# Recurrence of a bidirectional decay scan: the order of TensorE's transposes and matmuls, and of ScalarE's copies, within one iteration

## The chip, the cores and the metric

The kernel runs on one core of one Trainium2 chip. The metric is device microseconds of one execution; the time of a kernel is the median of several runs. The core has a matmul engine (TensorE, PE in the profile; PEld is its weight load), VectorE (DVE), ScalarE (ACT), GpSimd (POOL) and SyncE (SP), which issues most DMAs. Each engine works through its own instructions in order; semaphores tie them together. TensorE writes to PSUM banks, which the other engines read.

## The reference, cut to what matters

The computation is a gated bidirectional recurrence over 1024 tokens, on 4 sequences of 1024 channels, followed by two blocks of attention over 16 slots. Only the recurrence is touched.

```python
ek = exp(min(k, 30)); ekv = ek * k                    # v is k here
a[t] = a[t-1] * decay + ekv[t];  b[t] = b[t-1] * decay + ek[t]     # forward
# the same backward in time, giving nf, df, nb, db
num = nf + nb - ekv + exp(min(u + k, 30)) * k
den = df + db - ek  + exp(min(u + k, 30))
x = sigmoid(r) * (num / max(den, 1e-8)) * (0.8 + 0.2 * tf)
```

The first slot block needs, of each row of x, its sum of squares and its products with 16 vectors, and x itself in both layouts (tokens by channels, and turned).

## The kernel before, in words

The recurrence works on blocks of 128 channels by 1024 tokens, channels on partitions: `N = B * NK = 32` iterations, `i` over 4 sequences of 8 blocks. The loop is software-pipelined: iteration `i` holds the scans of block `i`, the quotient of block `i-1` and the transposes of block `i-2`. Nearly every instruction is pinned to program order (`pin`), so the order written in the loop is the order on each engine.

What each engine does in iteration `i`, in its order before the change:

- VectorE: forward scan of `ek` into the denominator half of `both[i]` (L320), forward scan of `ekv` into the numerator half (L320), backward scan of the denominator (L320, "both<-columns,edges,both"; it starts from `edge[0]`), the sum with the own term (L361, `den_sum`, needs `own[i]`), the quotient of block i-1 (L458, `newton`, needs `num_ps[i-1]` complete in PSUM), the own numerator (L374), and the backward scan of the numerator over pairs of tokens (L417, `numerator`, needs `pairs[i]` in PSUM and `edge[1]`).
- GpSimd: two products of block i-1 with its quotient guess (L447, L448), clamp and product for block i+1 (L302, L308), the floor of the denominator (L411, needs L361), and the last product of block i-1 into the gate (L471, needs L458).
- ScalarE: `own[i]` (L312), the two edges (L333: multiplications of one column; `edge[0]` from the end of the first scan, `edge[1]` from the end of the second), the copies of transposed blocks out of PSUM (L497, L529), the issue of the row store (L506), the quotient guess (L432 Ln, needs L411; L434 Exp), `ek` of block i+2 (L292), the square of block i-1 (L474) and the next decay matrix (L391).
- TensorE: transposes of block i-2 in two halves (L496, four 128x128 each), products of the squares of block i-2 (L482 "raw<-quo"), a block of weight work (L528 transposes, or L536 products, one item of the list `projection`), the pairs (L398, L399), the products of block i-1 (L482 "raw<-gate", needs L471), sometimes a half of a late transpose, and last the three sums of the numerator of block i (L382, `add_pairs`).

Every transposed half, every weight block and the pairs go through the same PSUM tile (`tag="ptr", bufs=1`), so each has to be read out by ScalarE (or, for the pairs, by L417) before the next is written. `own` and `num` have one PSUM buffer each as well; `both` has two, so the first scan of iteration i+1 waits until block i-1's L471 has read its buffer.

`HK = 4`: in iterations with `i % 4 == 0` the gates of four blocks go through one sigmoid (L279, 128x4096, with a table load on each side), and no transposes are done; the two halves that are left out are turned late, in the two iterations after the next. In iterations with `i % 4 == 1` there is a weight block and no late half, with 2 and 3 there are both. Iterations up to 3 have fewer blocks, as nothing is there yet.

## Time and profile before

| what | value |
|---|---|
| median of 3 runs | 1105.29 us (1103.33, 1105.29, 1107.35) |
| the profiled execution | 1108.89 us, of which the profiled span is 1107.1 us |
| busy in the span | PE 1002.8, PEld 552.3, VectorE 739.5, ScalarE 516.7, GpSimd 549.2 us |
| recurrence, first to last L417 | 20.31 to 406.94 us |
| idle of VectorE before L417 | 32.3 us in 15 places |
| idle of GpSimd before L447 in 87 to 394 us | 13.0 us |
| idle of TensorE before "raw<-gate" (L482) in 87 to 394 us | 34.1 us |

The span is what the profiler saw of one execution, 1.8 us shorter than that execution's time. "Busy" is a union of instruction times on an engine; durations of neighbours overlap by some tens of ns, so start-to-start distances are used where instructions follow each other. The table's first two rows are different executions: the profiled one took 3.6 us more than the median.

### The profile page before, as it was taken

How to read it: one execution, taken by the hardware profiler on the slowest of the kernel's cores; microseconds unless marked ns; L12 is line 12 of the kernel's file. 1: busy time of each engine (PE TensorE's matmuls, PEld its weight loads, DVE VectorE, ACT ScalarE, POOL GpSimd, SP SyncE). 2: the span in 40 equal slices, each digit the busy share in tenths (PEclk: the TensorE clock that was granted, in tenths of full speed). 3: DMA queues.
4: the chain of work that ended last, by engine and by line, in shares of the span. 5: the costliest groups of instructions: out<-in, count | busy, mean ns of one | idle time of the engine just before them, and what ended most of it. 6: DMA issues, size and time to landing. Idle time of an engine off the chain costs nothing.

```text
span 1107.1 us, 12203 instructions
## 1 busy us (share of the span) xinstructions
PE 1002.8 (91%) x4218; PEld 552.3 (50%) x4218; DVE 739.5 (67%) x1049; ACT 516.7 (47%) x818; POOL 549.2 (50%) x417
## 2 busy tenths in 40 slices
PE   4678888987888897899999999999899999999996
PEld 1223232322323242484666666765584667676764
DVE  7898898989898986233666656565233555555555
ACT  6576777667686753012343434334113333333332
POOL 4999898989898972200222222222100343444444
PEclk9899898989899899899999999999999999999999
DMA  8575464747464345591477777562771355555554
GB/s 271 177 258 190 144 212 136 262 138 247 152 209 120 108 139 200 168 407 59 169 265 256 262 283 271 204 207 99 270 288 40 142 200 193 206 190 209 190 203 158
DMA packets 121790, 218.81 MB, mean 198 GB/s; under 512 B 10928, under 2 KB 76592, under 8 KB 121728
## 3 DMA queue, kind: packets, MB, share of 16 engines
q1 hardware_dynamic: 87872, 199.15, 51.0%
q10 hardware_dynamic: 33280, 16.78, 5.1%
q0 software_dynamic: 576, 2.10, 0.5%
q8 instruction: 33, 0.54, 0.2%
q14 instruction: 29, 0.24, 0.1%
HBM read 150.90 MB, written 67.11 MB: 197 GB/s over the span
## 4 chain that ended last, share of the span: by engine, by line
PE 74%; DVE 12%; POOL 7%; ACT 3%; issue 2%; DMA 1%; SPq 1%; POOLq 0%; DVEq 0%; ACTq 0%
PE psc L1146 20%; PE po L1203 19%; DVE both L320 8%; PE raw L482 7%; PE num L382 4%; POOL gate L471 3%; PE ptr L1134 3%; PE pk L1006 3%; PE pkv L936 3%; PE pv L1074 2%; PE ptr L496 2%; DVE both L417 2%; PE pairs L398 2%; PE pw L886 1%; POOL both L411 1%
## 5 line engine op out<-in xcount | busy, mean ns | idle before, releaser
L1146 PE MATMUL psc<-km,xt 128*128 128x272 f32 (+1 forms) x1024 | 238.4, 386 | 0.0
L1203 PE MATMUL po<-vm,e 128*128 128x512 f32 x512 | 230.4, 593 | 0.9 <-ACT e L1193 0.9
L1146 PEld LDWEIGHTS psc<-km,xt 128*128 128x128 f32 x1024 | 189.5, 190 | 29.1
L1180 POOL TENSOR_TENSOR e<-e,den 128x256 f32<-128x256 f32 x64 | 40.6, 634 | 252.4 <-DVE den L1178 231.3
L1203 PEld LDWEIGHTS po<-vm,e 128*128 128x128 f32 x512 | 94.8, 190 | 95.7 <-issue 85.4
L482 PE MATMUL raw<-gate,lhs 128*32 128x512 f32 x128 | 74.7, 712 | 47.9 <-POOL gate L471 47.8
L1244 DVE SCALAR_TENSOR_TENSOR y<-y,inv,npost_bc 128x1024 f32<-128x1024 f32 x62 | 79.7, 1285 | 41.3 <-POOL inv L1239 41.3
L1212 DVE TENSOR_TENSOR y<-po,y 128x512 f32<-128x512 f32 x128 | 85.8, 674 | 31.0 <-PE po L1203 30.8
L1232 ACT ACTIVATE junk<-y 128x1024 f32<-128x1024 f32 x63 | 66.7, 1059 | 69.3 <-DVE y L1244 69.1
L447 POOL TENSOR_TENSOR both<-both,quo 128x1024 f32<-128x1024 f32 (+1 forms) x33 | 76.1, 2305 | 21.7 <-ACT quo L434 21.2
L1239 POOL TENSOR_TENSOR inv<-mean,minus_half 128x1 f32<-128x1 f32 x64 | 35.6, 557 | 96.7 <-DVE mean L1237 96.7
L382 PE MATMUL num<-both,ident 128*128 128x512 f32 x128 | 73.8, 702 | 6.3 <-DVE both L320 4.3
L308 POOL TENSOR_TENSOR ekv<-ek,kf 128x1024 f32<-128x1024 f32 (+1 forms) x33 | 76.1, 2308 | 2.6
L448 POOL TENSOR_TENSOR gate<-gate,quo 128x1024 f32<-128x1024 f32 (+1 forms) x33 | 76.9, 2329 | 0.0
L1193 ACT COPY e<-pet 128x256 f32<-128x256 f32 x64 | 23.8, 372 | 113.0 <-PE pet L1192 112.9
L320 DVE TENSOR_TENSOR_SCAN both<-columns,edges,both 128x1024 f32<-128x1024 f32 x32 | 74.4, 2325 | 1.8 <-ACT edges L333 1.8
L471 POOL TENSOR_TENSOR gate<-gate,both 128x1024 f32<-128x1024 f32 x31 | 73.7, 2377 | 1.1
L320 DVE TENSOR_TENSOR_SCAN both<-columns,ek 128x1024 f32<-128x1024 f32 (+1 forms) x32 | 71.8, 2243 | 3.5 <-POOL gate L471 3.3
L1341 POOL TENSOR_TENSOR y<-y,xin 128x1024 f32<-128x1024 f32 x31 | 73.1, 2359 | 1.4 <-DVE y L1244 1.4
L320 DVE TENSOR_TENSOR_SCAN both<-columns,ekv 128x1024 f32<-128x1024 f32 (+1 forms) x32 | 71.4, 2231 | 0.0
L1137 ACT COPY xt<-ptr 128x512 f32<-128x512 f32 x64 | 37.0, 577 | 70.2 <-PE ptr L1134 70.2
L1237 DVE TENSOR_SCALAR mean<-total 128x1 f32<-128x1 f32 x64 | 9.8, 154 | 85.2 <-ACT junk L1232 45.8
(212 smaller groups left out, 1639.8 us busy)
## 6 DMA issues: line engine op xcount, KB each, us to landing
y<-rows SPq DMA_DIRECT2D x64, 512.0 KB, 4.3
kf<-in_ft_dram SPq DMA_DIRECT2D x32, 512.0 KB, 5.3
gate<-in_xt_dram SPq DMA_DIRECT2D x32, 512.0 KB, 6.9
turned_rows<-gate SPq DMA_DIRECT2D x32, 512.0 KB, 3.6
xt<-turned_rows SPq DMA_DIRECT2D x32, 512.0 KB, 5.7
rows<-y SPq DMA_DIRECT2D x32, 512.0 KB, 2.9
xin<-in_x_dram SPq DMA_DIRECT2D x32, 512.0 KB, 4.6
rows<-stage ACTq DMA_DIRECT2D x31, 512.0 KB, 4.2
```

The lines of the kernel that those rows point to most:

```text
L308: pin(nc.gpsimd.tensor_tensor(ekv[:, part], ek[:, part], kf[:, part], ALU.mult))
L320: nc.vector.tensor_tensor_scan(dst[:, way], dec, src[:, way], start, ALU.mult, ALU.add)
L382: nc.tensor.matmul(num_ps[:, ts(h, 512)], by, src, start=False, stop=True, skip_group_check=True)
L447: pin(nc.gpsimd.tensor_tensor(den, den, quo[:, part], ALU.mult))
L448: pin(nc.gpsimd.tensor_tensor(xk, xk, quo[:, part], ALU.mult))
L471: pin(engine.tensor_tensor(xk, xk, factor[:, part], ALU.mult))
L482: nc.tensor.matmul(raw[rows_b, ts(h, 512)], lhs[:, w].rearrange("p h s -> p (h s)"), src[:, ts(h, 512)], start=(k == 0 and w == k), stop=( ...
L1146: nc.tensor.matmul(psc[g][:, :n], xt_g[g][:, k, :], maps["km"][:, g // NT, k, :n], start=(k == 0), stop=(k == NK - 1),)
L1203: nc.tensor.matmul(po, et[:, ts(c, P)], vm[:, c, ts(h, 512)], start=(c == 0), stop=(c == 1),)
L1212: pin(nc.vector.tensor_add(half, po, half))
L1244: pin(nc.vector.scalar_tensor_tensor(y[g], y[g], inv[g], npost_bc, ALU.mult, ALU.mult))
L1341: pin(nc.gpsimd.tensor_add(y[g - 1], y[g - 1], xin[g - 1]))
```

## The change

All edits lie in the loop of the recurrence. `sums_a` is split into `sums` (the two forward scans), `make_edge` and `denominator`; the transposes, weight blocks and their copies become pairs of closures, of which the first issues TensorE's part and returns the copy.

TensorE's order in an iteration with `i % 4 != 0` becomes: first half of block i-2, sum 0 and sum 1 of `num_ps[i-1]`, second half, sum 2, a third block (late half, or none), squares half 0, a fourth block (weights), squares half 1, pairs of block i, products of block i-1. The three sums (L382) move from the end of iteration i-1 to the beginning of iteration i, and the late half from the end of an iteration into the third place of the next. With `i % 4 == 0`: the three sums, the squares, the pairs, the products, as before.

ScalarE's order with `i % 4 != 0` becomes: copy 0, square of block i-2, `edge[0]`, copy 1 and the issue of the row store, `own[i]`, copy 2, `edge[1]`, copy 3, decay matrix of block i+1, guess (Ln, Exp), `ek` of block i+2. Before, it was: decay matrix, `own[i]`, `edge[0]` (those two exchanged with `i % 4 == 1`), late copy, `edge[1]`, copies 0 and 1, row store, weight copy, guess, `ek`, square. With `i % 4 == 0`: square, `own`, `edge[0]`, the sigmoid, `edge[1]`, decay matrix, guess.

VectorE's and GpSimd's orders are the same as before, and so is SyncE's; the gate loads of SyncE with `i % 4 == 3` wait for the late half, which stands later now.

```diff
+            adds = add_pairs(num_ps[i - 1], flat[i - 1], by[i - 1]) if past else [lambda: None] * 3
+            if i % HK == 0:
+                for fill in adds:
+                    fill()
+                if older:
+                    square(i - 2, quo[i - 2])
+                own_exp(i, kf[i], own[i])
+                make_edge(i, both[i], edge[i], 0)
...
+                gates(i // HK)
+                if past:
+                    make_edge(i, both[i], edge[i], 1)
+                    late_stage = staged(i - 2)
+                    contract(i - 2, quo[i - 2], NK)
+            else:
...
+                if older:
+                    stage = staged(i - 2)
+                    blocks = [rows_block(i - 2, h, stage) for h in range(2)]
+                if i > HK and i % HK > 1:
+                    blocks.append(rows_block(i - i % HK - 2, i % HK - 2, late_stage))
+                if i >= 3 and projection:
+                    blocks.append(projection.pop(0))
+                blocks = blocks[:2] + [None] * (4 - len(blocks)) + blocks[2:]
...
+                turn_block(0)
+                adds[0]()
+                copy[0]()
+                if older:
+                    square(i - 2, quo[i - 2])
+                adds[1]()
+                make_edge(i, both[i], edge[i], 0)
+                turn_block(1)
+                adds[2]()
+                copy[1]()
+                own_exp(i, kf[i], own[i])
+                turn_block(2)
+                if older:
+                    contract(i - 2, quo[i - 2], NK, (0,))
+                copy[2]()
+                make_edge(i, both[i], edge[i], 1)
+                turn_block(3)
+                if older:
+                    contract(i - 2, quo[i - 2], NK, (1,))
+                copy[3]()
+            denominator(i, both[i], edge[i])
+            if i < N - 1:
+                pairs[i] = make_pairs(i, both[i], by[i])
+            if i + 1 < N - 1:
+                by[i + 1] = decay_matrix(i + 1)
...
-            if older:
-                now = i % HK > 0
-                stage = staged(i - 2)
-                for h in range(2):
-                    if now:
-                        copy = turn_half(i - 2, h)
-                    contract(i - 2, quo[i - 2], NK, (h,))
-                    if now:
-                        copy(stage)
...
-            if i >= 3 and i % HK and projection:
-                projection.pop(0)()
-            if i < N - 1:
-                pairs[i] = make_pairs(i, both[i], by[i])
...
             if past:
-                square(i - 1, quo[i - 1])
-            if i + 1 < N - 1:
-                by[i + 1] = decay_matrix(i + 1)
-            if past:
                 contract(i - 1, gate_of(i - 1), (i - 1) % NK)
...
-            add_pairs(num_ps[i], flat[i], by[i])
```

The new helper that issues a half and returns its copy (the row store goes out with the second half):

```diff
+        def rows_block(i, h, stage):
+            def turn():
+                xk = gate_of(i)
+                ptr = rec_ps.tile([P, 4, P], F32, tag="ptr", bufs=1, name=f"ptr_{i}_{h}")
+                for q in range(4):
+                    pin(nc.tensor.transpose(ptr[:, q, :], xk[:, ts(4 * h + q, P)], ident))
+                return lambda: copy(ptr)
+
+            def copy(ptr):
+                pin(nc.scalar.copy(stage[:, 4 * h : 4 * h + 4, :], ptr))
+                if h == 1:
+                    send(i, stage)
+
+            return turn
```

More of the change, by code (lines that the diff above doesn't have):

```diff
@@ L323, in scan, with sums @@
             )
-        def sums_a(i, ek, ekv, parts, own_exp, between):
-            b, k = i // NK, i % NK
+        def sums(i, ek, ekv, parts):
             flat = rec.tile([P, 2 * L + 2], F32, tag="both", bufs=2, name=f"both_{i}")
             both = flat[:, : 2 * L].rearrange("p (n t) -> p n t", n=2)
-            edge = [edges[:, i % 8, :], flat[:, 2 * L : 2 * L + 1]]
-            def make_edge(n):
-                pin(nc.scalar.mul(edge[n], both[:, n, L - 1 : L], turn[:, b, k : k + 1]))
-            late = i % HK == 1
-            if not late:
-                own_exp()
             for n, src in enumerate((ek, ekv)):
@@ L345, in sums_a, with make_edge, denominator @@
                     )
-                if n == 0:
-                    make_edge(0)
-            if late:
-                own_exp()
-            if i == 0:
-                make_edge(1)
-            between()
-            if i > 0:
-                make_edge(1)
+            return flat, both, [edges[:, i % 8, :], flat[:, 2 * L : 2 * L + 1]]
+        def make_edge(i, both, edge, n):
+            b, k = i // NK, i % NK
+            pin(nc.scalar.mul(edge[n], both[:, n, L - 1 : L], turn[:, b, k : k + 1]))
+        def denominator(i, both, edge):
             den = both[:, 0, :]
             scan(den, den, i, edge[0], True)
-            return both, edge[1], flat
         def den_sum(both, own):
@@ L404, in add_pairs @@
             later = flat[:, L + 2 :].rearrange("p (s h) -> p h s", h=2)[:, 0]
-            add(num_ps, 0, f[:, 0])
-            add(num_ps, 1, f[:, 1])
-            add(num_ps, 1, later, by)
+            return [
+                lambda: add(num_ps, 0, f[:, 0]),
+                lambda: add(num_ps, 1, f[:, 1]),
+                lambda: add(num_ps, 1, later, by),
+            ]
         def floor(both):
@@ L417, in numerator @@
                 nc.vector.tensor_tensor_scan(
-                    even[:, ::-1], dec, pairs[:, ::-1], edge, ALU.mult, ALU.add
+                    even[:, ::-1], dec, pairs[:, ::-1], edge[1], ALU.mult, ALU.add
                 )
@@ L424, in numerator_half @@
             num = both[:, 1, ts(h, 512)]
-            scan(num, num, i, edge if h else both[:, 1, 512:513], True)
+            scan(num, num, i, edge[1] if h else both[:, 1, 512:513], True)
         def guess(i, both, parts=(every,)):
@@ L489, in contract @@
                 )
-        def turn_half(i, h):
-            xk = gate_of(i)
-            ptr = rec_ps.tile([P, 4, P], F32, tag="ptr", bufs=1, name=f"ptr_{i}_{h}")
-            for q in range(4):
-                pin(nc.tensor.transpose(ptr[:, q, :], xk[:, ts(4 * h + q, P)], ident))
-            return lambda stage: pin(nc.scalar.copy(stage[:, 4 * h : 4 * h + 4, :], ptr))
+        def rows_block(i, h, stage):
[10 more added lines that the diff above has]
+            return turn
         def staged(i):
@@ L528, in turn_weights @@
                 pin(nc.tensor.transpose(ptr[:, q, :], part[:, ts(q, P)], ident))
-            pin(nc.scalar.copy(part.rearrange("p (q c) -> p q c", c=P), ptr))
+            return lambda: pin(nc.scalar.copy(part.rearrange("p (q c) -> p q c", c=P), ptr))
         def group_products(j2):
@@ L543, in group_products @@
                     )
-            pin(nc.scalar.copy(wo_next[j2][:, :, :P], acc[:, :2, :]))
+            return lambda: pin(nc.scalar.copy(wo_next[j2][:, :, :P], acc[:, :2, :]))
         def group_sums():
@@ L553, in group_sums @@
                 )
-            pin(nc.scalar.copy(wo_cw.rearrange("p j s -> p (j s)"), pc))
+            return lambda: pin(nc.scalar.copy(wo_cw.rearrange("p j s -> p (j s)"), pc))
         projection = []
@@ L580 @@
         by[0] = decay_matrix(0)
-        late_copy = None
         for i in range(N):
@@ L588 @@
             own[i] = rec_ps.tile([P, L], F32, tag="own", bufs=1, name=f"own_{i}")
-            both[i], edge[i], flat[i] = sums_a(
-                i,
-                ek[i],
-                ekv[i],
-                [every] if past else halves,
-                lambda: own_exp(i, kf[i], own[i]),
-                lambda: gates(i // HK) if i % HK == 0 else late_copy() if late_copy else None,
-            )
-            late_copy = None
+            flat[i], both[i], edge[i] = sums(i, ek[i], ekv[i], [every] if past else halves)
@@ new lines, with turn_block @@
+            adds = add_pairs(num_ps[i - 1], flat[i - 1], by[i - 1]) if past else [lambda: None] * 3
[6 more added lines that the diff above has]
+                make_edge(i, both[i], edge[i], 0)
+                if i == 0:
+                    make_edge(i, both[i], edge[i], 1)
[5 more added lines that the diff above has]
+            else:
+                blocks = []
+                if older:
[6 more added lines that the diff above has]
+                blocks = blocks[:2] + [None] * (4 - len(blocks)) + blocks[2:]
+                copy = [None] * 4
+                def turn_block(n):
+                    copy[n] = blocks[n]() if blocks[n] else lambda: None
+                turn_block(0)
[13 more added lines that the diff above has]
+                copy[2]()
+                make_edge(i, both[i], edge[i], 1)
+                turn_block(3)
+                if older:
+                    contract(i - 2, quo[i - 2], NK, (1,))
+                copy[3]()
@@ L611 @@
                     load_ahead(0, n)
-            if older:
-                now = i % HK > 0
-                stage = staged(i - 2)
-                for h in range(2):
-                    if now:
-                        copy = turn_half(i - 2, h)
-                    contract(i - 2, quo[i - 2], NK, (h,))
-                    if now:
-                        copy(stage)
-                if now:
-                    send(i - 2, stage)
-                else:
-                    late_stage = stage
-            if i >= 3 and i % HK and projection:
-                projection.pop(0)()
-            if i < N - 1:
-                pairs[i] = make_pairs(i, both[i], by[i])
             if past:
@@ L652 @@
             if past:
-                square(i - 1, quo[i - 1])
-            if i + 1 < N - 1:
-                by[i + 1] = decay_matrix(i + 1)
-            if past:
                 contract(i - 1, gate_of(i - 1), (i - 1) % NK)
-            h = i % HK - 1
-            if i > HK and h in (0, 1):
-                j = i - i % HK - 2
-                copy = turn_half(j, h)
-                def late_copy(j=j, h=h, copy=copy, stage=late_stage):
-                    copy(stage)
-                    if h == 1:
-                        send(j, stage)
-            add_pairs(num_ps[i], flat[i], by[i])
         i = N - 1
```

## Prediction

> **What bounds the kernel now.** First the page: the chain of waits puts 74% on TensorE over the whole span, but that is the attention's share. The change touches the recurrence alone, so I read two stretches of it in the windows view (busy time per engine, then granted TensorE clock).

> ```profile
> 100.00:200.00 100.00, 85.96 (x259) 30.06 (x260) 89.94 (x55) 70.05 (x91) 90.34 (x48) 0.93 0.56 178
> 200.00:300.00 100.00, 85.26 (x262) 29.47 (x264) 90.04 (x55) 71.84 (x91) 91.46 (x47) 0.93 0.63 205
> ```

> TensorE, VectorE and GpSimd are each busy 85 to 91%: none is full, they wait for one another in turn, and the clock is below 1. Next the timeline of VectorE: L417, the numerator's scan, is its last instruction of an iteration.

> ```profile
> 265.27 1.28 DVE L417 TENSOR_TENSOR_SCAN both<-decay,both,pairs 128x512 f32<-128x512 f32 x1 [1.21 <-ACT quo L434]
> ...
> 276.77 1.27 DVE L417 TENSOR_TENSOR_SCAN both<-decay,both,pairs 128x512 f32<-128x512 f32 x1
> ...
> 291.96 1.28 DVE L417 TENSOR_TENSOR_SCAN both<-decay,both,pairs 128x512 f32<-128x512 f32 x1 [3.39 <-ACT quo L434]
> ...
> 303.61 1.28 DVE L417 TENSOR_TENSOR_SCAN both<-decay,both,pairs 128x512 f32<-128x512 f32 x1
> ...
> 316.43 1.28 DVE L417 TENSOR_TENSOR_SCAN both<-decay,both,pairs 128x512 f32<-128x512 f32 x1 [1.21 <-ACT quo L434]
> ```

> These are iterations 19 to 23. I call them K3, K0, K1, K2, K3 by `i % 4`: the steps are 11.50 (K0), 15.19 (K1), 11.65 (K2), 12.82 (K3), together 51.16 us. The releaser named is Exp, but the pairs end at the same moment (next fence: 290.79 + 1.06 = 291.85): L417 waits for pairs. Unhindered, an iteration takes 11.5 us on VectorE and 11.73 on GpSimd (253.59 to 265.32, without idle), so about 46.5 per four; the room is 4.6 us per group, some 30 us in all.

> ```profile
> 278.10 3.62 PE L482 MATMUL raw<-gate,lhs 128*32 128x512 f32 x4 [4.14 <-POOL gate L471]
> ...
> 289.14 0.59 ACT L529 COPY wp<-pwt 128x512 f32<-128x512 f32 x1 [0.98 <-PE pwt L528]
> 289.63 1.06 ACT L432 ACTIVATE quo<-both 128x1024 f32<-128x1024 f32 x1
> 289.78 1.17 PE L398 MATMUL pairs<-both,decay_matrix 128*128 128x512 f32 x2 [0.68 <-ACT wp L529]
> ...
> 292.01 2.37 POOL L447 TENSOR_TENSOR both<-both,quo 128x1024 f32<-128x1024 f32 x1 [2.26 <-ACT quo L434]
> ```

> That is K1: TensorE idles 4.14 us until L471, then its products take 3.62 instead of 1.90; the pairs wait 0.68 for the weight copy, and the guess behind that copy makes GpSimd idle too. The windows view, cut on a grid, shows why (second number: TensorE busy; seventh: clock).

> ```profile
> 72.00:75.41 3.41, 1.09 (x3) 0.36 (x4) 3.01 (x3) 3.38 (x5) 3.25 (x2) 1.00 0.05 16
> ...
> 198.29:201.71 3.42, 2.07 (x5) 0.67 (x4) 3.38 (x4) 2.28 (x3) 2.76 (x2) 1.00 0.51 153
> 273.39:276.80 3.41, 0.57 (x2) 0.00 (x0) 3.38 (x4) 3.27 (x5) 2.40 (x3) 1.00 0.01 2
> 276.80:280.21 3.41, 2.11 (x3) 0.54 (x4) 3.38 (x3) 3.39 (x4) 3.40 (x2) 0.50 0.32 101
> 280.21:283.63 3.42, 3.42 (x5) 0.94 (x4) 3.42 (x3) 1.59 (x3) 3.42 (x3) 0.50 0.71 205
> 454.29:457.71 3.42, 2.96 (x14) 2.16 (x14) 1.12 (x2) 0.37 (x1) 0.00 (x0) 0.50 0.02 5
> ```

> **The change, part by part.** Times below count from the start of an iteration's first scan (E); the products of the block before (raw<-gate) start there too, as both wait for L471.

> *TensorE's order.* The same matmuls, moved. In K2 and K3 (from the row at 253.66): products 1.83, half 0.49, two sums 4 x 0.45 = 1.80, so the second half starts at 4.12. The wait of 0.68 before the pairs is gone, as copy 3 lies under squares half 1. Without other waits the pairs would start at 8.60 (1.83 + 0.49 + 1.80 + 0.53 + 0.90 + 0.53 + 0.97 + 0.58 + 0.97), against 9.43 before (253.66 to 263.09).

> *ScalarE's order* gives half of that back. Copy 1 can begin 0.64 after its transposes (258.69 to 259.33): 4.76. The row store's issue follows 0.62 later and takes 0.37:

> ```profile
> L506 ACTq DMA_DIRECT2D rows<-stage x31: 366/366/399, 47.0 to 438.5; - x31
> ```

> So `own` starts at 5.80 and is there at 6.95; L361 wants it at 6.72: 0.23 late. Copy 2 is behind `own` (1.04 on: 6.84, 0.59 long), and the fourth block needs its bank: 7.48 instead of 7.04. Pairs at 9.04; with 2.18 to L417 (263.09 to 265.27) 11.22, and 1.20 to the next scan. K2 takes 12.42 (before 11.65, when its products had begun 1.38 ahead of the scan). L471 ends at 11.82, 0.6 before the next scan, so K3 has its products early: 10.66 + 1.20 = 11.86 (before 12.82). `edge[0]` is behind copy 0 and the square: 1.83 + 0.69 + 0.49 + 0.95 + 0.29 = 4.25, just in time for the backward scan at 4.36. [...]

> *K0* keeps its order: 11.62 (266.46 to 278.08). The decay matrix goes between `edge[1]` and Ln there: ScalarE is free at 275.5, so Ln slips from 275.68 to 275.8, 0.1, hidden in GpSimd's turn. Elsewhere it lies in the 0.5 us before the floor ends.

> *K1, the clock.* TensorE's gap before K1 shrinks from 4.14 to 3.2 (pairs end 8.63 after K0's products, which start 0.2 before the scan; next products at 11.64). A 3.2 gap leaves a window with at least 47% idle however it falls, and mostly over 68%, so halvings go on. With 5.5 us of half clock, as before, 2.75 are lost; now `own` and `edge[0]` sit behind TensorE: second half at 6.87, copy 7.51, `own` 8.55 to 9.70 (before: done at 3.6). L417 comes 3.68 after: 13.38, next scan 14.58 (before 15.08). The pairs are ready at 13.0, so the new wait replaces the old one and GpSimd's L471 ends only at 14.5 (11.67 before).

> *Sum.* A group at the same phase: 14.58 + 12.42 + 11.86 + 11.62 = 50.48, 0.7 under 51.2. To stay locked at 15 windows it would need 1.4 us more half clock: 6.9, where the most that two windows give is 6.83; close to that the first window is over 95% busy and releases early (half clock 3.1 to 3.4: 49.4). So the phases alternate, about 50.9, 49.4 and 49.4, mean 50: six groups from 87 to 394 us save 7.2. Against it: iteration 2 is caught by the clock at 38 us and its `own` is 2 us late, L417 about 1.0 later than 49.46; the block of group sums (L550, 1.96 us) in iteration 30 now lies on the path, 1.2. Sum -5.0. SyncE's gate loads, held up to 4 us longer by the late half, are needed five iterations later; the stores behind them wait for L471 anyway. The profiled execution is 1108.89 (span 1107.1 plus 1.8): 1103.9 for such a run; it lies 3.6 over the median, a spread of about one window, so I take the difference to the median: 1105.3 - 5.0 = 1100.3.

> [...]

> **Rivals.**
> (B) The lock holds: 15 windows per group whatever the order, each us gained before K1 turned into half clock. For it: five groups within 0.1 us of 51.2. Against: the 6.9 needed. The end shifts by the phase (-1.2) and iteration 30 (+1.2): 1105.
> (C) No halving at all: group 11.83 + 12.42 + 11.86 + 11.62 = 47.73, and 14 windows are 47.79, so a group whose gap is split in its middle stays there. It needs a window with 50 to 55% idle to pass, between the 39 and 68 of the rows. Five groups of 3.4 less 2.2: 1090.
> (D) Slower: `own` behind copy 1 and the row store becomes the bound. Place: ScalarE in K1, K2, K3. Price: every us that the issue holds ScalarE beyond 0.37 delays `own` or copy 2 in all three. It decides from 0.25 us more, which uses up the 0.7; at 0.5 a group is 51.3 to 52, with 2.2 from start and end about 1110.

> **Numbers.** A (forecast, 1097 to 1104) 0.40, B 0.25, C 0.12, D 0.23. Less than 0.3% (3.3 us) can't be told from no change here. Faster: C and 0.33 of A, 0.45. Same: the rest of A and nearly all of B, 0.30. Slower: D and 0.02, 0.25. Range for 8 in 10: from C's better part to D, 1089 to 1111; A's own is 1097 to 1104.

> **What would show it.** The wait before L398 gone (11.4 us in 87 to 394 before); L361 waiting for `own` in K1 by some 3 us, in K2 by 0.2; idle before L417 under 15 us (30); steps of L417 in a group near 14.6, 12.4, 11.9, 11.6; halvings at unequal distances. I am wrong if K2 and K3 exceed 12.6 each, if no halving is left, or if a group is still 51.2.

## The result, and the profile after

The changed kernel took 1099.92 us (median of 15 runs, 1095.37 to 1106.25) against 1105.29 for the kernel before; the ratio is 0.9951, with a 95% interval of 0.9935 to 0.9967. That is 5.4 us less, clear of no change, about half a per cent. Its profiled execution took 1100.06 us, with a span of 1098.3.

First the windows view, as before: length, then the busy time of TensorE, its weight load, VectorE, ScalarE and GpSimd, then the granted clock (and the DMA engines' share and rate).

```profile
100.00:200.00 100.00, 84.75 (x269) 29.48 (x266) 94.94 (x59) 74.69 (x95) 94.97 (x51) 0.98 0.57 179
200.00:300.00 100.00, 84.46 (x287) 30.12 (x287) 92.06 (x57) 72.08 (x92) 92.17 (x49) 0.95 0.64 210
```

VectorE and GpSimd are fuller (90 to 92-95%), and the clock is up from 0.93 to 0.95 and 0.98. Line numbers have moved: L408 is L417 of before, L341 is L333, L349 L361, L386 and L387 are L398 and L399, L462 is L471, L473 L482, L490 L496, L494 L497, L507 L506, L529 L528, L530 L529. The timeline of VectorE at the numerator's scan shows two groups of different length:

```profile
140.06 1.27 DVE L408 TENSOR_TENSOR_SCAN both<-decay,both,pairs 128x512 f32<-128x512 f32 x1
152.61 1.28 DVE L408 TENSOR_TENSOR_SCAN both<-decay,both,pairs 128x512 f32<-128x512 f32 x1 [0.59 <-PE pairs L387]
164.49 1.28 DVE L408 TENSOR_TENSOR_SCAN both<-decay,both,pairs 128x512 f32<-128x512 f32 x1 [0.21 <-PE pairs L387]
176.00 1.27 DVE L408 TENSOR_TENSOR_SCAN both<-decay,both,pairs 128x512 f32<-128x512 f32 x1
187.86 1.27 DVE L408 TENSOR_TENSOR_SCAN both<-decay,both,pairs 128x512 f32<-128x512 f32 x1
...
273.86 1.27 DVE L408 TENSOR_TENSOR_SCAN both<-decay,both,pairs 128x512 f32<-128x512 f32 x1
288.62 1.27 DVE L408 TENSOR_TENSOR_SCAN both<-decay,both,pairs 128x512 f32<-128x512 f32 x1
```

K2 takes 12.55, K3 11.88, K0 11.51; K1 is 11.86 (176.00 to 187.86) where the clock stayed up and 14.76 (273.86 to 288.62) where it halved for two windows. All distances, in ordinary numbers (from the L417 or L408 of iteration 5, that is `i % 4 == 1`, to that of 29):

```
group of four        1      2      3      4      5      6     mean
before             51.30  51.14  51.22  51.16  51.18  51.25  51.21
after              49.29  47.80  50.05  50.71  49.43  47.81  49.18
 of it K2 + K3     24.44  24.43  25.06  24.45  24.46  24.44
 of it K1          13.35  11.86  13.48  14.76  13.34  11.86
```

K2 + K3 took 24.47 in most groups before (11.57 + 12.90). So nothing was won there, nor in K0; the gain is all in K1, which took 15.2 to 15.3. In this execution's trace the clock goes from 1.00 to 0.50 at 52.56, 76.45, 127.66, 226.64, 274.43, 325.62 and 397.31 between 50 and 400 us: distances of 7, 15, 29, 14, 15 and 21 times 3.413. The windows view, cut on that grid, says why K1 differs:

```profile
124.25:127.66 3.41, 0.62 (x2) 0.00 (x0) 3.38 (x4) 3.37 (x5) 3.28 (x3) 1.00 0.00 0
172.03:175.44 3.41, 2.13 (x5) 0.67 (x4) 3.34 (x4) 3.38 (x5) 3.30 (x3) 1.00 0.04 15
175.44:178.86 3.42, 1.54 (x4) 0.36 (x4) 3.39 (x3) 3.04 (x3) 3.07 (x2) 1.00 0.16 53
178.86:182.27 3.41, 3.41 (x14) 1.83 (x14) 3.41 (x3) 1.90 (x4) 3.41 (x2) 1.00 0.83 255
...
270.99:274.43 3.44, 1.03 (x3) 0.16 (x1) 3.41 (x4) 3.38 (x6) 3.31 (x3) 1.00 0.38 157
```

The gap of TensorE before K1 is 3.16 us in these three groups (in all six: 3.16, 3.16, 3.67, 3.16, 3.00 and 3.17). Most of it falls into one window at 127.66 and 274.43 (0.62 and 1.03 us busy: half clock follows), and it is split at 175.44 (2.13 and 1.54 busy: no half clock). The third, fourth and fifth gaps were followed by half clock as the first was; the second and the sixth were not. What K1 costs when the clock halves for two windows stands in the timeline of all engines:

```profile
275.18 3.62 PE L473 MATMUL raw<-gate,lhs 128*32 128x512 f32 x4 [3.16 <-POOL gate L462]
...
279.89 0.59 ACT L494 COPY stage<-ptr 128x512 f32<-128x512 f32 x1 [3.52 <-PE ptr L490]
...
281.65 2.35 DVE L320 TENSOR_TENSOR_SCAN both<-columns,edges,both 128x1024 f32<-128x1024 f32 x1 [2.01 <-ACT edges L341]
...
283.46 0.37 ACTq L507 DMA_DIRECT2D rows<-stage  x1
...
283.88 1.12 ACT L312 ACTIVATE own<-kf,u_sb 128x1024 f32<-128x1024 f32 x1 [0.44 <-ACT stage L494]
...
285.03 1.22 DVE L349 SCALAR_TENSOR_TENSOR both<-own,both 128x1024 f32<-128x1024 f32 x1 [1.03 <-ACT own L312]
```

ScalarE waits 3.52 us for the first half with `edge[0]` and `own` queued behind the copy: the backward scan starts 2.01 late and the sum with `own` 1.03 more, the new wait that stands where the wait for pairs was.

The two profiled spans differ by 8.8 us, more than the medians. By sections: to L408 of iteration 5 +3.6, the six groups -12.2, iteration 30 +3.0 (12.55 to 15.55), and -3.3 behind the recurrence. That last part goes with the clock in an untouched stage: before, it was halved at 454.30 for two windows; after, it was not, and 3.0 of the 3.3 us arise between the matmuls just ahead of that moment and those just behind it (starts 451.57 and 467.88 before, 445.59 and 458.86 after).

### The profile page after: what moved, and what is told of

The parts are those of the page before. It is cut to its first block, busy times and chain, and to the rows that moved or that the text cites. A ratio compares the mean times of both kernels' runs of the same rounds, so it can differ in the third digit from the quotient of the medians.

```text
span 1098.3 us, 12246 instructions
## 1 busy us (share of the span) xinstructions
PE 990.5 (90%) x4218; PEld 548.8 (50%) x4218; DVE 740.3 (67%) x1049; ACT 517.7 (47%) x818; POOL 548.2 (50%) x417
## 4 chain that ended last, share of the span: by engine, by line
PE 68%; POOL 11%; DVE 9%; ACT 6%; issue 3%; DMA 1%; SPq 1%; ACTq 0%; POOLq 0%; DVEq 0%
PE psc L1162 20%; PE po L1219 19%; PE raw L473 5%; DVE both L320 4%; POOL gate L462 4%; PE num L370 3%; PE ptr L1150 3%; PE pk L1022 3%; PE pkv L952 3%; PE pv L1090 2%; POOL both L402 2%; POOL gate L439 2%; PE ptr L490 2%; POOL ekv L308 1%; DVE both L349 1%
## 5 line engine op out<-in xcount | busy, mean ns | idle before, releaser
L473 PE MATMUL raw<-gate,lhs 128*32 128x512 f32 x128 | 72.1, 690 | 59.8 <-POOL gate L462 59.8
L1228 DVE TENSOR_TENSOR y<-po,y 128x512 f32<-128x512 f32 x128 | 85.9, 675 | 30.2 <-PE po L1219 29.9
L370 PE MATMUL num<-both,ident 128*128 128x512 f32 x128 | 68.4, 656 | 7.0 <-DVE both L320 5.0
L462 POOL TENSOR_TENSOR gate<-gate,both 128x1024 f32<-128x1024 f32 x31 | 73.6, 2374 | 1.6
L473 PEld LDWEIGHTS raw<-gate,lhs 128*32 128x32 f32 x128 | 12.6, 118 | 112.5 <-POOL gate L462 85.0
```

The source lines that it names most:

```text
L370: nc.tensor.matmul(num_ps[:, ts(h, 512)], by, src, start=False, stop=True, skip_group_check=True)
L462: pin(engine.tensor_tensor(xk, xk, factor[:, part], ALU.mult))
L473: nc.tensor.matmul(raw[rows_b, ts(h, 512)], lhs[:, w].rearrange("p h s -> p (h s)"), src[:, ts(h, 512)], start=(k == 0 and w == k), stop=( ...
L1228: pin(nc.vector.tensor_add(half, po, half))
```

## The experiments

Times are medians, the ratio is that to runs of the kernel before on the same chip (whose median was 1107.80 for the first four, 1105.31 for the next four, 1107.35 for the last two; the changed kernel's is 0.9951).

**1 and 2: the gap filled, in the changed kernel and in the one before.** Three or four spare matmuls behind the pairs of iterations with `i % 4 == 0`, into columns that nothing reads:

```diff
             if i < N - 1:
                 pairs[i] = make_pairs(i, both[i], by[i])
+            if i % HK == 0 and i >= HK:
+                for _ in range(3):              # 4 in the kernel before
+                    pin(nc.tensor.matmul(columns[:, 128:], ident, npost_bc[:, :384], start=True, stop=True))
```

> The changed kernel with three spare 128x384 matmuls behind the pairs of every iteration with i % 4 == 0 (from 4 on), into the free part of the columns bank, so that TensorE's idle before K1 falls from 3.2 to about 1.2 us. Theory (the clock decides): no halving between 90 and 390 us, every group of four 47.7 to 47.8 us instead of 49.2 on average, L349 never waits more than 0.3 us for own; six groups save 9 us: about 1091 us. Rival (the shorter way to the pairs made the gain, and lost clock lies beside other waits): within 2 us of 1099.9, groups of 49 us.

> The kernel before with four such spare matmuls behind the pairs of iterations with i % 4 == 0 (its idle there is 4.1 us; about 1.4 stay). Theory (the clock decides): no halving, no lock; K1 12.3, K2 12.1, K3 12.3, K0 11.6, group 48.3 instead of 51.2: 17 us less, about 1088, so that the order of the change is worth 0.6 us per group without the clock and the two filled kernels are within 4 us of each other. Rival (the order makes the gain): stays 5 us or more above the filled changed kernel.

Measured: 1091.29 (0.9873, 0.9846 to 0.9900) and 1090.54 (0.9862, 0.9839 to 0.9885). There was no halving between 90 and 390 us in either, as the windows view shows (first the changed kernel, then the one before; the clock is the 1.00):

```profile
90.00:390.00 300.00, 265.12 (x891) 98.26 (x890) 286.88 (x176) 224.72 (x286) 288.54 (x151) 1.00 0.57 181
90.00:390.00 300.00, 269.10 (x891) 100.61 (x891) 283.67 (x174) 222.51 (x283) 286.08 (x150) 1.00 0.56 178
```

Groups took 47.81 to 48.19 (mean 47.98) and 48.53 to 48.66 (48.59). Both came as the theory had it, within 0.3 us a group on average. The second is the more telling: the old order with four spare matmuls beats the change by some 9 us, and with the clock up the two orders can't be told apart: the new one gains 0.6 a group, 3.7 in all, and loses 1.8 up to iteration 5 and 0.8 in iteration 30. That gain, too, lies in K1, which takes 11.84 to 11.87 in the new order and 12.54 to 12.67 in the old one.

In the kernel before, the trace named Exp as what L417 waited for, but the pairs ended at the same moment, as the row that the prediction reads shows:

```profile
290.79 1.06 PE L399 MATMUL pairs<-both,ident 128*128 128x512 f32 x2
```

The waits view of the kernel before with the filled gap, 85 to 395 us (waiting engine and line, releaser; total, times, longest), shows that both its waits are still there, the one of L417 at about half (30.2 without the filling), the one for the weight copy nearly whole (10.1):

```profile
DVE both L417 <- PE pairs L399: 13.2, 19, 0.9
...
PE pairs L398 <- ACT wp L529: 9.5, 14, 0.7
```

So the wait for the weight copy was not what made a group 51.2 us long, and about half of L417's wait went with the half clock alone.

**5 and 10: the gap of the kernel before shortened to the new length.** One matmul of 480 columns instead of four of 384, nothing else.

> The kernel before with one spare 128x480 matmul (0.85 us) behind the pairs of iterations with i % 4 == 0, so that TensorE's idle before K1 is 3.3 us, as in the changed kernel, with the old order otherwise. Theory (the length of that gap decides how often the clock halves and for how long): the lock at 15 windows is broken, groups between 48.6 (no halving), 50 (one window) and 51.2 (two windows), mean about 50: 6 us less than before, about 1099. Rival (only the new order breaks the lock; a gap of 3.3 still halves it every time for two windows): groups 51.2, within 2 us of before.

> The kernel before with the one spare 128x480 matmul once more, for a profile of another execution: its first profiled execution was the slowest of six and locked in four groups of 51.2. Theory: in an execution near the median (1096) fewer than half of the groups are 51.2 and the others are 48.6 to 50.3. Rival (it stays locked, and the time came from elsewhere): five or six groups at 51.2 at a time near 1096.

Measured: 1096.60 (0.9925, 0.9908 to 0.9942), a little below the change itself, though the two intervals touch. Experiment 10 is a single execution, so it counts for its trace alone. The first profile was of the slowest execution (1103.65) and is locked in four of six groups: 50.24, 51.23, 51.26, 51.18, 51.19, 48.59. The second (1095.85) has 50.26, 48.52, 50.25, 48.52, 50.11, 48.59: a halving of one window in every second group and none in the others, as the theory has it. The lock can thus still be met with a gap of 3.3, but it need not be: of the two executions profiled one had it. In the windows view of the two (first profile, then second), the last window before half clock and two that were passed:

```profile
270.97:274.38 3.41, 1.33 (x4) 0.29 (x2) 3.38 (x4) 3.27 (x5) 2.41 (x3) 1.00 0.00 0
```

```profile
168.00:171.34 3.34, 1.75 (x5) 0.45 (x3) 3.27 (x4) 3.23 (x4) 2.34 (x3) 1.00 0.00 0
171.34:174.75 3.41, 1.67 (x4) 0.36 (x4) 3.38 (x3) 3.38 (x4) 3.40 (x2) 1.00 0.20 65
```

A window 39% busy was followed by half clock; a gap split into two windows of 52 and 49% was not.

**4: the last copy uncovered.**

```diff
-                turn_block(3)
                 if older:
                     contract(i - 2, quo[i - 2], NK, (1,))
+                turn_block(3)
                 copy[3]()
```

> The changed kernel with the fourth block behind the squares of half 1 instead of ahead of them: its copy is no longer covered, and the pairs wait for it again. Theory: pairs 0.7 later in K2 and K3, the wait before the pairs back at 0.6 to 0.7 in each such iteration, K2 + K3 0.9 to 1.4 longer, K1 the same: 5 to 8 us more than 1099.9, unless the grid takes part of it. Rival (the cover of the last copy is worth nothing, since ScalarE's order holds TensorE up anyway): within 2 us of 1099.9.

Measured: 1101.71 (0.9945, 0.9924 to 0.9966), no different from the change within these intervals. The theory's 5 to 8 us are not there: the rival holds. The wait came back as expected, in the waits view of this kernel, 85 to 395 us (first line); the second line is from that view of the changed kernel:

```profile
PE pairs L386 <- ACT wp L530: 10.1, 15, 0.7
...
PE pwt L529 <- ACT stage L494: 4.3, 10, 0.4
```

but K2 + K3 stayed at 24.3 (12.32 + 11.96). In the changed kernel the fourth block had to wait 0.43 us for copy 2 behind `own`, and the squares behind it; with the block last that wait is gone, and most of the 0.68 before the pairs is made up (in one K2 the pairs start 9.18 us after the products instead of 9.05). So covering the wait before the pairs, the most visible edit of the change, was worth nothing in K2 and K3. In K1 it may be worth some 0.2 us (13.57 to 13.95 with a short halving against 13.34 to 13.48, 14.94 with a long one against 14.76); K1 without a halving isn't among these groups, whose mean is 49.8.

**3: the row store behind `own`.**

```diff
-                    blocks = [rows_block(i - 2, h, stage) for h in range(2)]
+                    blocks = [rows_block(i - 2, h, stage, False) for h in range(2)]
...
                 copy[1]()
                 own_exp(i, kf[i], own[i])
+                if older:
+                    send(i - 2, stage)
```

The `False` leaves the store out of the copy.

> The changed kernel with the issue of the row store (second half of block i-2) behind own instead of ahead of it. If the issue holds ScalarE for its 0.37 us as in the trace: own begins 0.45 earlier, L349's wait for own falls from 5.7 us to under 2, copy 2 comes at the same time as before, groups 0.2 to 0.4 shorter: 1 to 3 us less than 1099.9. If it holds ScalarE much longer than its row shows (rival D of the prediction): 5 us or more.

Measured: 1093.21 (0.9882, 0.9859 to 0.9906), 7 us below the change rather than 1 to 3. That is the size which the expectation kept for an issue that holds ScalarE longer than its row shows, but the row still says 0.37. ScalarE's timeline in this kernel shows what I had not seen:

```profile
205.03 0.59 ACT L494 COPY stage<-ptr 128x512 f32<-128x512 f32 x1 [0.52 <-PE ptr L490]
205.52 1.12 ACT L312 ACTIVATE own<-kf,u_sb 128x1024 f32<-128x1024 f32 x1
205.65 0.37 ACTq L507 DMA_DIRECT2D rows<-stage  x1
206.57 0.59 ACT L494 COPY stage<-ptr 128x512 f32<-128x512 f32 x1
```

In the changed kernel the same copy runs from 206.17 to 206.75, the issue starts at 206.79 and `own`, behind it, at 207.20, with 0.44 of idle put down to that copy. With `own` in between, `own` starts at 205.52, 0.49 after the copy's start instead of 1.03; the issue runs beside it at 205.65; and copy 2 starts 1.05 after `own` (1.06 in the changed kernel), not 0.4 later as I had it. So, counted from the copy, `own` and copy 2 are both about half a microsecond earlier. K2 fell from 12.55 to 11.8-12.1 in four groups (one of the others had a halving), the mean group from 49.18 to 48.48, and the wait of L349 for `own` all but went (waits view, 85 to 395 us, of the changed kernel and of this one):

```profile
DVE both L349 <- ACT own L312: 5.7, 14, 1.0
DVE both L349 <- ACT own L312: 0.3, 1, 0.3
```

Of the 7.7 us between the two profiled spans 4.2 are in the groups, and 2.4 in iteration 30, which met no half clock this time. So not all of the 7 us is the store's.

**6: `own` and `edge[0]` ahead of copy 0.**

```diff
+                own_exp(i, kf[i], own[i])
+                make_edge(i, both[i], edge[i], 0)
                 turn_block(0)
                 adds[0]()
                 copy[0]()
...
                 adds[1]()
-                make_edge(i, both[i], edge[i], 0)
...
                 copy[1]()
-                own_exp(i, kf[i], own[i])
```

> The changed kernel with own and edge 0 ahead of copy 0 on ScalarE (which idles there, waiting for the first half), the rest as in the change. Theory (what the change gives back is own and edge 0 behind TensorE's blocks): L349 and the backward scan wait for ScalarE no more; K2 + K3 23.7 instead of 24.45, K1 11.7 without a halving, 13.2 with a short one; group about 47.8: about 1092. Rival (these waits lie beside the wait for pairs): within 2 us of 1099.9.

Measured: 1093.78 (0.9904, 0.9883 to 0.9924). Near the theory's 1092: both waits are gone, K2 + K3 is 23.6 (11.51 + 12.05) in the last three groups, K1 11.76 without a halving and 13.2 to 13.3 with a short one. But two groups had a long one (14.4): the gaps before K1 were 3.08 (no halving), 3.07 and 4.37 (long ones) and three times 3.25 (short ones), so it was again chiefly their place on the grid that decided. The mean group was 48.9, against the 47.8 expected.

**7, 8 and 9: together.**

> The store behind own, and three spare matmuls in the gap as in the first filled kernel. If both gains add: no halving in 90 to 390 us, K2 11.9, K3 11.8, K0 11.5, K1 11.75, group 47.0; about 1086. If GpSimd's 11.73 per iteration or the store's gain with halvings only (K1) takes it up: 47.5 or more, 1090.

> Own and edge 0 ahead of copy 0, and three spare matmuls in the gap. The bound is then GpSimd, 11.73 per iteration: group 46.9 to 47.1, no halving in 90 to 390 us; about 1085. If edge 0's early place gains nothing over the store behind own once the clock stays up, it equals the filled kernel with the late store.

> Own and edge 0 ahead of copy 0, three spare matmuls in the gap, and the block of group sums (L551, sixteen matmuls 16 columns wide) in iteration 31, where no pairs follow, instead of 30. Theory: iteration 30 loses the 1.4 us by which the block is longer than a weight block, and a window filled with these narrow matmuls is not followed by half clock there: step from L408 of 29 to 30 12.2 instead of 13.65, 1.5 us less than the kernel without the move: about 1082. Rival: the tail waits for the sums or their copy in iteration 31 instead, no difference within 1 us.

The seventh is experiment 3 with the three spare matmuls of experiment 1, the eighth experiment 6 with them. The ninth moves the group sums out of iteration 30 and adds to the eighth:

```diff
-                if i >= 3 and projection:
+                if i >= 3 and projection and i != N - 2:
```

Measured: 1086.78 (0.9829, 0.9814 to 0.9845), 1083.65 (0.9816, 0.9791 to 0.9840) and 1084.37 (0.9807, 0.9768 to 0.9847); mean groups 47.4, 47.3 and 47.3. Most of the two gains adds up: by the ratios, filling gives 0.8% and the late store 0.7%, together 1.2%; with `own` first (0.5%) the two give 1.35%. So the causes are largely separate. The seventh's time is the theory's 1086, but its mean group is nearer to the 47.5 of its rival than to 47.0. The 46.9 of GpSimd alone isn't reached, K2 keeping 12.0 to 12.7. In the ninth the step from iteration 29 to 30 fell from 13.65 to 11.97, as expected; the medians can't tell it from the eighth. Experiments 7 to 9 beat both kernels by over 1%, and which of the three is best stays open.

## Why the prediction was right, step by step

- *The room and the lock.* Right. Six groups of 51.14 to 51.30 became 47.8 to 50.7, and experiments 1, 2, 5 and 10 show that TensorE's gap decides it, by its length and by where it falls on the grid, with the order left alone.
- *K0, K2, K3.* 11.62, 12.42, 11.86 forecast; 11.50, 12.55, 11.89 measured in four of the six groups. The 0.23 by which `own` would be late is 0.26 in the waits of L349. But the text let the covered wait count as a gain of 0.2 in K2 + K3; measured is none, and experiment 4 shows that the cover itself is worth nothing there.
- *K1.* 14.58 with 5.5 us of half clock; 14.76 measured in the one long case, with 6.1. The 3 us by which L361 was to wait for `own` there are 2.01 for `edge[0]` and then 1.03 for `own`. Groups with a short halving: 49.4 forecast, 49.29 and 49.43. Without: 47.73 as rival C had it; 47.80 and 47.81.
- *The mean group.* 50 forecast, 49.18 measured: 12.2 us saved, not 7.2. This term was mis-sized. I had the passing of a window at 50 to 55% idle as an unlikely extra (0.12). Over the traces of the recurrence in these kernels, narrow matmuls aside (last section), every full-clock window up to 1.34 us busy (39%) was followed by half clock; above that both happened: 1.40 (41%, at 26.76 in experiment 1) and 1.46 (43%, at 328.38 in experiment 3) were followed by it, 1.49 (44%, at 373.41 in the changed kernel) was not; and 1.54 (45%) passed at 175.44. So the gap of 3.16 that was split near its middle passed. What decides within that strip stays open. Rival C's state was met in two groups of six, for one group at a time.
- *Start and iteration 30.* 2.2 forecast; 6.6 in this execution (3.6 and 3.0). Mis-sized too: the clock also halved at 52.56, in iteration 3, after a gap of 2.44, and at 397.31 in iteration 30.
- *The sum.* -5.0 forecast, -5.4 between the medians, but -8.8 between the profiles. Two errors of 4 to 5 us nearly cancelled, and 3.3 us of the profiles' difference lies behind the recurrence, where the clock's phase differs. That the sum came so close was luck; that the lock broke, and through K1, was not.
- *Rival D* named the right place, ScalarE's `own` behind copy 1 and the store, but its price did not come, as the issue did not hold longer than its 0.37; that it delays what is behind it by about 0.5 in all was in the sum, that a neighbour could hide it was not.
- *The gap's length.* Gaps of 3.00 to 3.16 us before K1 were followed by half clock here in three groups of six, one of 3.67 in a fourth, and one of 2.44 in iteration 3; gaps of 3.16 and 3.17 in the other two groups were not. So length alone didn't decide here; the busy share of the windows measured went with the outcome.

## What to carry to other kernels

Where a group of iterations keeps one length (here 51.14 to 51.30 six times, 15 times 3.413), look for a grid: cut the windows view on the times at which the clock changes, and read the busy share of each window. In the changed kernel the gaps of TensorE before K1 were all 3.00 to 3.67 us long; half clock followed where they left a window with 1.03 us busy or less, and not where the emptiest had 1.49 or 1.54. So look at what share of a window a pause empties. A few spare matmuls in it cost a line and here gave more than a reordering (ratios of 0.9873 and 0.9862 against 0.9951). ScalarE's rows here come in the order of the program; work that waits for nothing, put between a copy and the DMA issue that needs its result, began half a microsecond earlier (experiment 3), and put ahead of copies that wait for TensorE it took K2 + K3 from 24.45 to 23.6 (experiment 6). Both are worth trying elsewhere.

## What the hardware showed that was not expected

The clock's release: in the changed kernel a window at half clock with 2.66 of 3.41 us busy (78%, at 274.43) was followed by another at half clock, one with 3.00 (88%, at 325.62) and one with 3.05 (89%, at 127.66) by full clock. In experiment 4 one with 2.72 (80%, at 175.50) was followed by full clock too. A window with 2.96 (87%) at 454.29 in the kernel before was not; it held ten matmuls of 64 columns.

Windows with narrow matmuls did not go with their busy share as the others did. The windows view of the changed kernel in iteration 30, where sixteen matmuls of 16 columns ran (1.96 us), and that of the kernel before where 32 matmuls of 64 columns began:

```profile
393.90:397.31 3.41, 2.98 (x20) 2.00 (x18) 3.12 (x4) 1.28 (x4) 3.28 (x3) 1.00 0.48 134
```

```profile
450.88:454.29 3.41, 2.72 (x25) 2.75 (x25) 0.00 (x0) 0.00 (x0) 0.23 (x1) 1.00 0.31 126
```

Both were followed by half clock at 87 and 80% busy, where in the recurrence 45% had passed. Without the sixteen, the first window has 1.02 us of other matmuls. In experiments 5 and 10 such a window (3.05 us busy, at 397.26 and 389.81) had 1.09 beside them and was followed by half clock as well; in 8 the sixteen also lay in one window (377.87), with 1.45 beside them, and it was not. So in these four windows the outcome went with the rest of the window; that the sixteen count for less is my reading of them. Nor did the 64-column matmuls always bring half clock: in the changed kernel a window of nothing else was not followed by it at 2.91 us (85%):

```profile
445.09:448.50 3.41, 2.91 (x26) 2.94 (x27) 0.00 (x0) 0.00 (x0) 0.65 (x1) 1.00 0.23 93
```

The width was not tried by itself in any run.
